# A two-layer typed graph transformer on one core: edge rows in a ring of 48 slots, one write behind each gather

## The chip, the core and the metric

The kernel runs on one core of a Trainium2 chip. The metric is device time in microseconds for one launch, the median of several runs. The core has five engines that work through their own queues in order: TensorE (PE), VectorE (DVE), ScalarE (ACT), GpSimd (POOL) and SyncE (SP). They meet at semaphores. Transfers between HBM and the on-chip memory SBUF run on 16 DMA engines; in this kernel every indexed transfer (a gather or a scatter with one row index per partition) is issued by POOL, every plain one inside the layers by SP. PSUM is the small memory that PE writes to and that DVE and ACT can read and write.

## What is computed

A graph of 6250 nodes and 100000 edges, 128 features, 8 heads of 16, 16 node types, 32 edge types, two layers:

```python
k, q, v = typed_linear(x, ntype, Wk), ...          # one 128x128 matrix per node type
kT = einsum('nhd,htdo->nhto', k, Watt)             # per node: a key for each edge type
vT = einsum('nhd,htdo->nhto', v, Wmsg)             # per node: a value for each edge type
kw, m = kT[src, :, etype], vT[src, :, etype]       # one row per edge
a = einsum('ehd,ehd->eh', kw, q[dst]) * pri[:, etype].T / SQRT_D
att = edge_softmax(a, dst, n)                      # softmax over the edges into a node
hag = segment_sum(m * att[:, :, None], dst)        # sum over the edges into a node
h = silu(typed_linear(hag, ntype, Wa))
h = layernorm(h * alpha + x * (1 - alpha)) * g + b
```

After two layers come a linear map, the residual with the input and a last normalisation.

## The kernel before

The keys and values of every node for all 32 edge types are written to a table in HBM, one for each layer (`tabs[l]`). A row of it holds 128 key values and 128 value values in f32, 1 KB. Nodes are sorted into 49 bins of 128 nodes, one node per partition, so that the nodes of a bin have about the same number of incoming edges. A bin has a fixed number of slots K (`KB`): 25, 21, 19, 18, 17, 16, 15, 15, 14, 12, 11 for the own bins of each of four groups of node types, and 42, 20, 16, 14, 9 for mixed bins. The slots of all bins add up to 833. Bins go by superblocks of two to four.

`edges(l)` does the attention of a layer. For each slot of a bin one gather on POOL (L1136) brings 128 table rows, one per partition. Behind each gather stand two small writes on POOL into a tile `pause` that nobody reads (L1140). POOL's order is the order in which the program is written; the other engines' queues are put in order by a scheduler. A chunk is a tile `kv` of up to four slots, out of twelve such tiles (48 slots of 1 KB per partition). For each chunk DVE multiplies the keys by the query in place (L1150) and sums each head (L1154) into `a`.

When all chunks of a bin are through, `finished` runs step by step between the chunks of the next bin: mask, maximum, exponential on ACT, denominator (L1042 to L1055), then for each chunk the values times the weights (L1066) and an addition into an accumulator of four rows (L1073), and at last the sum over these four rows (L1076). The accumulator, the weights and the query lie in SBUF in the first layer and in PSUM in the second. A tile `kv` is free for new gathers when its values are added.

`nodes` makes the rest of a superblock (normalisation of the sums L1188, transposes L231, typed linear maps L223 with masked inputs from DVE L209, layer norm), and in the first layer the keys, values and queries of the next one (L1302, L1283) and, through `table_block` (PE L246, copies on ACT L253 or DVE L251), the blocks of the second table, which POOL scatters to HBM (L1349), two scatters per bin. In the second layer POOL scatters the results (L1382). This work is put between the chunks: `step` advances `finished` by one step, `tick(n)` advances the work of earlier superblocks by the share that n slots stand for, `leave` counts the chunks until a result is written. Before, a chunk of c slots has three points with `step` and `tick(c / 3)`.

The second layer's first gather waits for all scatters of the table. The phase ahead of the layers sorts the edges, and makes the first table (scatters L893).

Of the kernel before, what the change touches and what calls it, by code (L numbers as in the profile page):

```python
# [9 lines left out]
F32 = mybir.dt.float32  # L10
BF16 = mybir.dt.bfloat16
# [17 lines left out]

BINS = P // NC  # L30

CH = 4


def bins_of_degrees(lam):
# [27 lines left out]
def kernel(  # L63
# [45 lines left out]
    assert max(KB) * H + P <= 512 and max(KB) <= P and min(KB) >= CH and NR >= NP and NB <= P and TY == NC * TC  # L109

    WIN = SB * P
    LO, HI = windows_of_types(N, NP - N, TY, WIN)
# [810 lines left out]
    def arm(fast):  # L923

        puts = []

        outs_put, results = [], []
        STB = 3 if fast else 2
        ep = ctx2.enter_context(tc.tile_pool(name="ep", bufs=2))
        npl = ctx2.enter_context(tc.tile_pool(name="npl", bufs=1))  # L930
        eps = npl.tile([P, 1], F32, name="eps")
        nc.vector.memset(eps, LN_EPS)

# [54 lines left out]
        def edges(l):  # L988
# [47 lines left out]
            def finished(s, i, chunks, kvt, a, pair, sums, den):  # L1036
# [12 lines left out]
                nc.vector.tensor_tensor(av, av, m.unsqueeze(1).to_broadcast([P, K, H]),  # L1049
                                        op=ALU.subtract)  # L1050
                w = av if l == 0 else pair[:, 1, D:D + K * H].rearrange("p (k h) -> p k h", h=H)
                nc.scalar.activation(w, av, AF.Exp)
                yield
                yield
                nc.vector.tensor_reduce(den[:, i, :], w.rearrange("p k h -> p h k"),  # L1055
                                        axis=AX.X, op=ALU.add)

                if l == 0:
                    acc = ep.tile([P, CH, D], F32, name="acc", bufs=1)
                else:  # L1060
                    acc = pair[:, 0].rearrange("p (k c) -> p k c", k=CH)
                for j in range(len(chunks) + 1):
                    if j < len(chunks):
                        j0, j1 = chunks[j]
                        v = kvt[j][:, :j1 - j0, D:]
                        nc.vector.tensor_tensor(  # L1066
                            (v if j else acc).rearrange("p k (h d) -> p k h d", h=H),
                            v.rearrange("p k (h d) -> p k h d", h=H),
                            w[:, j0:j1, :].unsqueeze(3).to_broadcast([P, j1 - j0, H, HS]),
                            op=ALU.mult)  # L1070
                    if j > 1:
                        j0, j1 = chunks[j - 1]
                        nc.vector.tensor_tensor(acc[:, :j1 - j0], kvt[j - 1][:, :j1 - j0, D:],  # L1073
                                                acc[:, :j1 - j0], op=ALU.add)
                    yield
                nc.vector.tensor_reduce(sums[:, i, :], acc.rearrange("p k c -> p c k"),  # L1076
                                        axis=AX.X, op=ALU.add)
# [13 lines left out]
            def table(s, gen):  # L1091
# [5 lines left out]
                else:  # L1097
                    tables[s] = gen
                    spread(pieces, gen, 8 * sbs[s][1] + 4, (1.0 if s + 4 < len(sbs) else 0.6) * slots(min(s + 2, len(sbs) - 1)))

            before = iter(())
            q, pair = query(0, 0)
            for s, (i0, k, types) in enumerate(sbs):
# [7 lines left out]
                for i in range(k):  # L1111
                    b = i0 + i
                    K = KB[b]
                    a = ep.tile([P, max(KB), H], F32, name="a")
                    chunks = [(j, min(j + CH, K)) for j in range(0, K, CH)]
                    kvt = []
                    then = []

                    def step(end=False):
# [9 lines left out]
                    for j0, j1 in chunks:  # L1129
                        c = j1 - j0  # L1130
                        kv = ep.tile([P, CH, 2 * D], F32, name="kv", bufs=12)
                        kvt.append(kv)
                        pause = ep.tile([P, CH, 2, SB * H], F32, name="pause", bufs=2)
                        for j in range(j0, j1):
                            at = KO[b] + j
                            get = nc.gpsimd.indirect_dma_start(  # L1136
                                out=kv[:, j - j0, :], out_offset=None, in_=tabs[l][:],
                                in_offset=bass.IndirectOffsetOnAxis(ap=ell[:, at:at + 1], axis=0))
                            for half in range(2):
                                nc.gpsimd.memset(pause[:, j - j0, half], 0.0)  # L1140
# [8 lines left out]
                        kk = kv[:, :c, :D]  # L1149
                        nc.vector.tensor_tensor(  # L1150
                            kk, kk, q.unsqueeze(1).to_broadcast([P, c, D]), op=ALU.mult)
                        step()
                        tick(c / 3)
                        nc.vector.tensor_reduce(a[:, j0:j1, :],  # L1154
                                                kk.rearrange("p k (h d) -> p k h d", h=H),
                                                axis=AX.X, op=ALU.add)
# [9 lines left out]
                    before = finished(s, i, chunks, kvt, a, pair, sums, den)  # L1166
                    q, pair = then[0] if then else (None, None)
            for _ in before:
                pass
# [53 lines left out]
        def nodes(l, i0, k, types, sums, den, ntb, table):  # L1223
# [326 lines left out]
```

## Time and profile before

Three runs took 3612.12, 3613.41 and 3602.87 us. The profiled execution took 3602.11 us, with a span of 3600.3 us.

| engine | busy us | share of the span | instructions |
|---|---|---|---|
| PE | 1776.3 | 49% | 5529 |
| DVE | 1905.3 | 53% | 4273 |
| ACT | 981.2 | 27% | 1599 |
| POOL | 2444.3 | 68% | 5483 |

How to read what follows. A row of a group names the line, the engine, the operation, what is written and read, the shape and the count; behind the bar stand the busy time in us and the mean of one instruction in ns; behind the second bar the time that the engine stood idle just before these instructions, and what ended it. "issue" is idle time in which nothing that the profile shows was waited for. A row of waits gives the total in us, the number of waits and the longest. A row of the timeline gives start, duration, engine, line and operation, with the idle time ahead of it in brackets. A row of a stage gives its limits and length in us, then busy time and count for PE, PE's weight loads, DVE, ACT and POOL, the granted clock of PE, the share of the DMA engines and GB/s.

### The profile page before, as it was taken

How to read it: one execution, taken by the hardware profiler on the slowest of the kernel's cores; microseconds unless marked ns; L12 is line 12 of the kernel's file. 1: busy time of each engine (PE TensorE's matmuls, PEld its weight loads, DVE VectorE, ACT ScalarE, POOL GpSimd, SP SyncE). 2: the span in 40 equal slices, each digit the busy share in tenths (PEclk: the TensorE clock that was granted, in tenths of full speed). 3: DMA queues.
4: the chain of work that ended last, by engine and by line, in shares of the span. 5: the costliest groups of instructions: out<-in, count | busy, mean ns of one | idle time of the engine just before them, and what ended most of it. 6: DMA issues, size and time to landing. Idle time of an engine off the chain costs nothing. (4 is left out here: it accounts for less than half of the span.)

```text
span 3600.3 us, 25278 instructions
## 1 busy us (share of the span) xinstructions
PE 1776.3 (49%) x5529; PEld 810.8 (23%) x5529; DVE 1905.3 (53%) x4273; ACT 981.2 (27%) x1599; POOL 2444.3 (68%) x5483
## 2 busy tenths in 40 slices
PE   4899889501775676546776669201201202113013
PEld 2455344300221232222222223101101101111012
DVE  8647423146544564446555552346556555556554
ACT  1556556300432243212342336101111101111111
POOL 1222466588688866688688771588888878888883
PEclk8769777555766686566776667655555555555555
DMA  5678899943655665354685569533333333333331
GB/s 139 289 303 338 334 378 411 356 100 95 222 205 207 236 237 214 133 205 147 218 321 185 179 245 363 203 94 102 98 99 98 100 88 103 97 97 98 99 97 39
DMA packets 189545, 681.72 MB, mean 189 GB/s; under 512 B 53964, under 2 KB 103278, under 8 KB 164334
## 3 DMA queue, kind: packets, MB, share of 16 engines
q0 software_dynamic: 115456, 642.08, 49.6%
q1 hardware_dynamic: 57538, 30.77, 3.2%
q10 hardware_dynamic: 16384, 7.11, 0.9%
q8 instruction: 48, 0.79, 0.1%
q14 instruction: 119, 0.97, 0.1%
HBM read 255.52 MB, written 425.02 MB: 189 GB/s over the span
## 5 line engine op out<-in xcount | busy, mean ns | idle before, releaser
L1136 POOL DMA_INDIRECT kv<-tab,ell x1666 | 1677.6, 1007 | 401.3 <-issue 303.4
L253 ACT COPY st<-tb 128x512 f32<-128x512 f32 (+1 forms) x1016 | 699.4, 758 | 671.2 <-PE tb L246 339.7
L231 PE MATMUL nb<-ident,hag 128*128 128x128 f32 x98 | 25.8, 406 | 754.1 <-DVE hag L1188 403.0
L1140 POOL MEMSET pause<- 128x32 f32 x3332 | 347.2, 141 | 40.7 <-issue 28.0
L1150 DVE TENSOR_TENSOR kv<-kv,tb 128x512 f32<-128x512 f32 (+3 forms) x227 | 145.4, 640 | 394.6 <-DMA kv<-tab,ell 382.5
L246 PE MATMUL tb<-bdv,kvT 32*128 32x512 f32 x784 | 290.6, 850 | 115.7 <-ACT st L253 69.0
L246 PE MATMUL tb<-bdk,kvT 32*128 32x512 f32 x784 | 280.6, 846 | 56.0 <-ACT st L253 34.9
L893 POOL DMA_INDIRECT tab<-st,rows x98 | 101.9, 1040 | 298.1 <-ACT st L253 232.2
L1154 DVE TENSOR_REDUCE a<-kv 128x32 f32<-128x512 f32 (+3 forms) x454 | 286.8, 635 | 3.6 <-DVE tb L1066 0.7
L246 PE MATMUL tb<-bdv,vT 32*128 32x512 f32 x784 | 275.8, 830 | 15.2 <-ACT st L253 8.0
L209 DVE SCALAR_TENSOR_TENSOR xm<-ntb,nb 128x512 f32<-128x512 bf16 (+2 forms) x288 | 157.5, 585 | 220.8 <-remote 66.0
L1150 DVE TENSOR_TENSOR kv<-kv,q 128x512 f32<-128x512 f32 (+3 forms) x227 | 145.4, 643 | 230.6 <-DMA kv<-tab,ell 220.0
L1349 POOL DMA_INDIRECT tab<-st,row x98 | 106.5, 1087 | 221.0 <-ACT st L253 186.5
L223 PE MATMUL nb<-xm,wa 128*128 128x512 f32 (+2 forms) x320 | 192.3, 752 | 112.8 <-DVE xm L209 73.3
L246 PE MATMUL tb<-bdk,kT 32*128 32x512 f32 x784 | 232.5, 825 | 1.5 <-ACT st L253 0.7
L251 DVE COPY st<-tb 128x512 f32<-128x512 f32 (+1 forms) x160 | 116.5, 730 | 210.1 <-PE tb L246 164.5
L231 PEld LDWEIGHTS nb<-ident,hag 128*128 128x128 f32 x98 | 15.9, 202 | 773.3 <-issue 598.8
L223 PE MATMUL nb<-xm,wq 128*128 128x512 f32 (+2 forms) x160 | 98.7, 765 | 156.9 <-DVE a L1042 91.9
L231 PE MATMUL nb<-ident,hs 128*128 128x128 f32 x98 | 36.0, 462 | 232.8 <-DVE hs L1261 174.3
L1302 PE MATMUL nb<-xm,wkqv 128*128 128x512 f32 (+1 forms) x288 | 144.7, 660 | 9.0 <-DVE xm L209 9.0
L1033 ACT COPY tb<-q 128x128 f32<-128x128 f32 x49 | 13.2, 269 | 454.2 <-DVE sums L1076 280.7
L246 PEld LDWEIGHTS tb<-bdv,kvT 32*128 32x128 f32 x784 | 79.7, 237 | 243.1 <-ACT st L253 134.4
(284 smaller groups left out, 2924.9 us busy)
## 6 DMA issues: line engine op xcount, KB each, us to landing
kv<-tab,ell POOLq DMA_INDIRECT x1666
hr<-xrd SPq DMA_DIRECT2D x24, 256.0 KB
hr<-xrd SPq DMA_DIRECT2D x15, 192.0 KB
xrd<-xr POOLq DMA_DIRECT2D x10, 256.0 KB
ntb<-typed SPq DMA_DIRECT2D x16, 128.0 KB
hrd<-hs SPq DMA_DIRECT2D x8, 256.0 KB
qrd<-q SPq DMA_DIRECT2D x8, 256.0 KB
q<-qrd SPq DMA_DIRECT2D x8, 256.0 KB
```

The costliest lines, as they stand in the source:

```text
L209: nc.vector.scalar_tensor_tensor(xm[:, :n], ntb[:, :n], float(t), hT[:, :n], op0=ALU.is_equal, op1=ALU.mult)
L223: nc.tensor.matmul(ps[:, :n], w[:, t, :], xm[:, :n], start=(t == types[0]), stop=(t == types[-1]))
L246: nc.tensor.matmul(pt[:, b], yT[s, i * P:(i + 1) * P], bd[s, tt, :], start=True, stop=True)
L251: nc.vector.tensor_copy(to, pt)
L253: nc.scalar.copy(to, pt)
L893: put = nc.gpsimd.indirect_dma_start(out=tabs[0].rearrange("(n t) c -> n (t c)", t=16), out_offset=bass.IndirectOffsetOnAxis(ap=rows1[:, t ...
L1136: get = nc.gpsimd.indirect_dma_start(out=kv[:, j - j0, :], out_offset=None, in_=tabs[l][:], in_offset=bass.IndirectOffsetOnAxis(ap=ell[:, ...
L1140: nc.gpsimd.memset(pause[:, j - j0, half], 0.0)
L1150: nc.vector.tensor_tensor(kk, kk, q.unsqueeze(1).to_broadcast([P, c, D]), op=ALU.mult)
L1154: nc.vector.tensor_reduce(a[:, j0:j1, :], kk.rearrange("p k (h d) -> p k h d", h=H), axis=AX.X, op=ALU.add)
L1302: nc.tensor.matmul(ps[:, :n], wkqv[:, j, t, :], xm[:, :n], start=(t == types[0]), stop=(t == types[-1]))
L1349: put = nc.gpsimd.indirect_dma_start(out=tabs[1].rearrange("(n t) c -> n (t c)", t=16), out_offset=bass.IndirectOffsetOnAxis(ap=row2[:, tg ...
```

## The change

Edge rows now lie in one tile `rows` of 48 slots that is used as a ring. `cut` divides a bin's K slots into chunks as even as can be, of at most eight, and cuts a chunk where the ring ends. `unread` holds the slots whose values are not yet summed; before a gather is written into such a slot, `finished` of the bin before is advanced. In `finished` each chunk's weighted values are summed over their slots by one instruction into a row of `part`, and the rows of `part` are summed at the end, in SBUF in both layers. A chunk has five points with `step` and `tick(c / 5)`. Behind each gather stands one write of 64 bf16 elements instead of two of 32 f32. Result rows are written after 4 + i chunks, not 7 + 2 i.

```diff
-CH = 4
+CH = 8
+RING = 48
...
+            ring["rows"] = npl.tile([P, RING, 2 * D], F32, name="rows")
...
-                if l == 0:
-                    acc = ep.tile([P, CH, D], F32, name="acc", bufs=1)
-                else:
-                    acc = pair[:, 0].rearrange("p (k c) -> p k c", k=CH)
-                for j in range(len(chunks) + 1):
-                    if j < len(chunks):
-                        j0, j1 = chunks[j]
-                        v = kvt[j][:, :j1 - j0, D:]
-                        nc.vector.tensor_tensor(
-                            (v if j else acc).rearrange("p k (h d) -> p k h d", h=H),
-                            v.rearrange("p k (h d) -> p k h d", h=H),
-                            w[:, j0:j1, :].unsqueeze(3).to_broadcast([P, j1 - j0, H, HS]),
-                            op=ALU.mult)
-                    if j > 1:
-                        j0, j1 = chunks[j - 1]
-                        nc.vector.tensor_tensor(acc[:, :j1 - j0], kvt[j - 1][:, :j1 - j0, D:],
-                                                acc[:, :j1 - j0], op=ALU.add)
-                    yield
-                nc.vector.tensor_reduce(sums[:, i, :], acc.rearrange("p k c -> p c k"),
+                part = ep.tile([P, PARTS, D], F32, name="part", bufs=1)
+                for j, (j0, j1, v, sl) in enumerate(chunks):
+                    nc.vector.tensor_tensor(
+                        v.rearrange("p k (h d) -> p k h d", h=H),
+                        v.rearrange("p k (h d) -> p k h d", h=H),
+                        w[:, j0:j1, :].unsqueeze(3).to_broadcast([P, j1 - j0, H, HS]),
+                        op=ALU.mult)
                     yield
+                    nc.vector.tensor_reduce(part[:, j, :], v.rearrange("p k c -> p c k"),
+                                            axis=AX.X, op=ALU.add)
+                    unread.difference_update(sl)
+                    yield
+                nc.vector.tensor_reduce(sums[:, i, :],
+                                        part[:, :len(chunks)].rearrange("p k c -> p c k"),
                                         axis=AX.X, op=ALU.add)
...
+            def cut(K):
+                cuts, j = [], 0
+                while j < K:
+                    most = -(-(K - j) // -(-(K - j) // CH))
+                    c = min(most, RING - ring["at"])
+                    sl = range(ring["at"], ring["at"] + c)
+                    cuts.append((j, j + c, ring["rows"][:, sl.start:sl.stop, :], sl))
+                    ring["at"] = sl.stop % RING
+                    j += c
+                return cuts
...
-                    chunks = [(j, min(j + CH, K)) for j in range(0, K, CH)]
+                    chunks = cut(K)
...
-                        kv = ep.tile([P, CH, 2 * D], F32, name="kv", bufs=12)
-                        pause = ep.tile([P, CH, 2, SB * H], F32, name="pause", bufs=2)
+                        while not unread.isdisjoint(sl):
+                            step()
+                        unread.update(sl)
+                        pause = ep.tile([P, CH, SB * BINS // 2], BF16, name="pause", bufs=2)
...
-                            for half in range(2):
-                                nc.gpsimd.memset(pause[:, j - j0, half], 0.0)
+                            nc.gpsimd.memset(pause[:, j - j0], 0.0)
...
-                        step()
-                        tick(c / 3)
+                        for _ in range(2):
+                            step()
+                            tick(c / 5)
                         nc.vector.tensor_reduce(a[:, j0:j1, :],
...
-                        step()
-                        tick(c / 3)
-                        step()
-                        tick(c / 3)
+                        for _ in range(3):
+                            step()
+                            tick(c / 5)
...
-                    results.append([7 + 2 * i, (o, i0, i)])
+                    results.append([4 + i, (o, i0, i)])
```

More of the change, by code (lines that the diff above doesn't have):

```diff
@@ L108 @@
     assert D == P and H * HS == D and H == 8 and HS == 16 and EC % J == 0 and NP > N and L == 2
-    assert max(KB) * H + P <= 512 and max(KB) <= P and min(KB) >= CH and NR >= NP and NB <= P and TY == NC * TC
+    assert max(KB) * H + P <= 512 and max(KB) <= P and RING >= max(KB) and NR >= NP and NB <= P and TY == NC * TC
     WIN = SB * P
@@ L927, in arm @@
         outs_put, results = [], []
+        PARTS = -(-max(KB) // CH) + 1
         STB = 3 if fast else 2
@@ L930, in arm @@
         npl = ctx2.enter_context(tc.tile_pool(name="npl", bufs=1))
+        ring = {"at": 0}
+        if fast:
+            ring["rows"] = npl.tile([P, RING, 2 * D], F32, name="rows")
         eps = npl.tile([P, 1], F32, name="eps")
@@ L1034, in query, with finished @@
                 return pair[:, 1, :D], pair
-            def finished(s, i, chunks, kvt, a, pair, sums, den):
+            def finished(s, i, chunks, a, pair, sums, den):
                 i0, k, _ = sbs[s]
@@ L1099, in table @@
                     spread(pieces, gen, 8 * sbs[s][1] + 4, (1.0 if s + 4 < len(sbs) else 0.6) * slots(min(s + 2, len(sbs) - 1)))
+            def cut(K):
[7 more added lines that the diff above has]
+                    j += c
+                assert len(cuts) <= PARTS
+                return cuts
+            unread = set()
             before = iter(())
@@ L1127, in step @@
                                 then.append(query(s + 1, 0))
-                    for j0, j1 in chunks:
+                    for j0, j1, kv, sl in chunks:
                         c = j1 - j0
-                        kv = ep.tile([P, CH, 2 * D], F32, name="kv", bufs=12)
-                        kvt.append(kv)
-                        pause = ep.tile([P, CH, 2, SB * H], F32, name="pause", bufs=2)
+                        while not unread.isdisjoint(sl):
+                            step()
+                        unread.update(sl)
+                        pause = ep.tile([P, CH, SB * BINS // 2], BF16, name="pause", bufs=2)
                         for j in range(j0, j1):
@@ L1165, in edges @@
                         step(end=True)
-                    before = finished(s, i, chunks, kvt, a, pair, sums, den)
+                    before = finished(s, i, [(j0, j1, kv[:, :, D:], sl) for j0, j1, kv, sl in chunks],
+                                      a, pair, sums, den)
                     q, pair = then[0] if then else (None, None)
```

3 lines of the change are left out of this document (1 added, 2 removed).

## The prediction

> **What bounds the kernel now.** I read the page's shares first, then busy time by stage, then POOL's groups and waits in each stage, then the timeline of a few gathers. The trace gives four stages from the kernel's lines: the first layer's gathers (704 to 2177 us), the table scatters left after them, the second layer's gathers (2293 to 3542), and the tail.
>
> ```profile
> span 3600.3 us, 25278 instructions
> ...
> POOL 1222466588688866688688771588888878888883
> ...
> 704.00:2177.00 1473.00, 877.36 (x2320) 338.86 (x2321) 800.80 (x1694) 423.69 (x563) 1135.48 (x2578) 0.66 0.58 197
> 2177.00:2293.00 116.00, 91.63 (x344) 35.87 (x342) 29.69 (x56) 67.03 (x82) 18.95 (x20) 0.75 0.90 369
> 2293.00:3542.00 1249.00, 215.43 (x538) 124.11 (x538) 696.26 (x1664) 130.45 (x263) 1015.10 (x2539) 0.53 0.33 97
> 3542.00:3600.00 58.00, 23.16 (x63) 14.73 (x63) 23.68 (x82) 11.26 (x17) 7.35 (x10) 0.53 0.05 16
> ```
>
> The columns are PE, PE's weight loads, DVE, ACT and POOL busy time. In the second layer POOL is busy 1015 of 1249 us and DVE 696; nothing else comes near. POOL's groups there, then in the first layer:
>
> ```profile
> L1136 POOL DMA_INDIRECT kv<-tab,ell x833 | 799.9, 960 | 197.4 <-issue 160.9 <-DMA tab<-st,row 9.0 <-DVE tb L1066 7.5
> L1140 POOL MEMSET pause<- 128x32 f32 x1664 | 174.9, 140 | 31.4 <-issue 24.4 <-POOL pause L1140 0.2
> ...
> L1136 POOL DMA_INDIRECT kv<-tab,ell x833 | 877.8, 1054 | 203.9 <-issue 142.5 <-DVE acc L1066 40.4 <-SPq L1546 8.8
> L1140 POOL MEMSET pause<- 128x32 f32 x1666 | 172.1, 142 | 9.3 <-issue 3.6 <-remote 3.6 <-POOL pause L1140 0.2
> L1349 POOL DMA_INDIRECT tab<-st,row x79 | 88.0, 1114 | 129.3 <-ACT st L253 113.7 <-issue 11.6 <-ACT a L1052 3.9
> ```
>
> In the second layer the first two groups with their idle time make 1204 of the 1249 us, and most of that idle time (185 of 229) is "issue", not another engine: POOL's instruction stream sets this stage. In the first layer 114 us pass while its scatters wait for ACT's table copies. There PE (877 of 1473 us) and ACT make the tables, and POOL is only one of two paces.
>
> **The change part by part.** *The write behind a gather.* A gather now repeats like this:
>
> ```profile
> 2401.21 0.20 POOL L1140 MEMSET pause<- 128x32 f32 x2
> 2401.57 0.95 POOL L1136 DMA_INDIRECT kv<-tab,ell  x1 [0.15 <-issue]
> 2402.52 0.21 POOL L1140 MEMSET pause<- 128x32 f32 x2
> 2402.88 0.95 POOL L1136 DMA_INDIRECT kv<-tab,ell  x1 [0.15 <-issue]
> ```
>
> So 0.95 + 0.20 + 0.15 = 1.31 us from gather to gather. Two writes of 0.14 overlap to 0.20: the second costs only 0.06. The trace also has gathers with no write between them, and longer writes:
>
> ```profile
> 102.62 0.97 POOL L847 DMA_INDIRECT xg<-in_x_dram,inv  x1 [0.30 <-issue]
> 103.89 0.95 POOL L847 DMA_INDIRECT xg<-in_x_dram,inv  x1 [0.30 <-issue]
> 105.14 0.95 POOL L847 DMA_INDIRECT xg<-in_x_dram,inv  x1 [0.30 <-issue]
> ...
> L858 POOL MEMSET kT<- 128x197 f32 x1 | 0.3, 278 | 0.0
> ```
>
> Without any write the step is 1.25 us: 0.30 passes between two gathers anyhow, and the writes stand mostly inside it. One write as long as now gives 0.95 + 0.14 + 0.15 = 1.24, or that 1.25. But the one write is 64 bf16 elements, not 32 f32 (the same 128 bytes), and no bf16 write on POOL is in the trace. If elements count and not bytes, it costs (278 - 140) / (197 - 32) = 0.84 ns for each of 32 more, 0.167 us, and the step is 1.27. The ends are therefore 0.04 and 0.07 us saved; I take 0.055, between the two. Per layer that is 833 x 0.055 = 46 us (33 to 58).
>
> The Trainium skill (VectorE: DVE Perf Modes, Zero memsets can be issued as uint32) says that a memset costs a cycle per element whatever the type, on VectorE; if POOL followed it, the write would be the longer one and this term 33 us a layer instead of 46. No run here shows it yet.
>
> *Fewer instructions on POOL.* Beyond the regular 0.154 us, "issue" holds irregular stalls, such as this one:
>
> ```profile
> 2419.84 0.12 POOL L1140 MEMSET pause<- 128x32 f32 x1 [0.18 <-issue]
> 2420.55 0.13 POOL L1140 MEMSET pause<- 128x32 f32 x1 [0.58 <-issue]
> 2421.45 0.95 POOL L1136 DMA_INDIRECT kv<-tab,ell  x1 [0.78 <-issue]
> ...
> POOL kv L1136 <- issue: 160.9, 724, 1.5
> POOL pause L1140 <- issue: 24.4, 62, 1.3
> ...
> POOL kv L1136 <- issue: 142.5, 778, 1.5
> POOL tab L1349 <- ACT st L253: 113.7, 20, 19.6
> POOL kv L1136 <- DVE acc L1066: 40.4, 3, 23.6
> ```
>
> Layer two (first two waits): 160.9 - 724 x 0.154 + 24.4 = 74 us; layer one: 142.5 - 778 x 0.154 + 3.6 = 26 us. I don't know what they wait for. If they come by the number of instructions, one of three instructions per gather goes and a third of the stalls (25 and 9 us); if by time or by gather, nothing. I take half of that: 12 and 4 us.
>
> *The ring.* Before, a bin of 42 rows takes 11 of the 12 tiles of four, which leaves 4 rows of lead; now 48 - 42 = 6, given back by chunk. In the order of the two programs, the gather with the shortest lead over the gather on whose sums it waits has a lead of 1 in the second layer before (its wait on DVE is the 7.5 us above) and 7 after; most others have 14 or more in both. In the first layer the shortest lead is 5 before and 3 after (the 49th gather, once). So the ring takes away the 7.5 us in the second layer (0 to 9), and about nothing in the first; the 40.4 us there come from a DVE that itself stands behind PE, which the ring doesn't touch:
>
> ```profile
> 1389.41 0.56 DVE L209 SCALAR_TENSOR_TENSOR xm<-ntb,nb 128x384 f32<-128x384 bf16 x1 [14.49 <-PE tb L246]
> ```
>
> The table scatters come one or two gathers later in POOL's order, the result writes about five earlier: no cost.
>
> *VectorE.* The two layers have 454 chunks before and 271 after, over the same 1666 rows of 128 values.
>
> ```profile
> L1154 DVE TENSOR_REDUCE a<-kv 128x32 f32<-128x512 f32 x376 | 254.8, 678 | 2.3 <-DVE a L1049 0.3 <-DVE kv L1066 0.3
> L1154 DVE TENSOR_REDUCE a<-kv 128x8 f32<-128x128 f32 x26 | 7.3, 279 | 0.1
> L1076 DVE TENSOR_REDUCE sums<-acc 128x128 f32<-128x512 f32 x49 | 51.3, 1048 | 1.2 <-DVE hs L1261 0.9
> L1076 DVE TENSOR_REDUCE sums<-tb 128x128 f32<-128x512 f32 x49 | 33.4, 682 | 1.3 <-DVE t L1205 1.3
> L1073 DVE TENSOR_TENSOR tb<-kv,tb 128x512 f32<-128x512 f32 (+3 forms) x174 | 109.5, 629 | 0.0
> L1073 DVE TENSOR_TENSOR acc<-kv,acc 128x512 f32<-128x512 f32 (+3 forms) x176 | 110.1, 626 | 0.3
> ```
>
> From the first two rows an instruction costs 0.146 us and 1.04 ns per element. The sum over rows of acc in SBUF, which steps from row to row, costs (1048 - 146) / 512 = 1.76 ns; from PSUM it costs the plain rate. The new sum of a chunk steps through SBUF in both layers. Per layer it costs 833 x 128 x 1.76 ns + 135 x 0.146 = 208 us (131 at the plain rate); the sum over the parts adds about 38. Out go the adds (110), the old last sum (50 and 33) and 3 x 91 x 0.146 = 40 of fixed cost. DVE so has about 46 us more in the first layer and 63 in the second. At 696 + 63 = 759 us of some 1180 it stays well under POOL, and the lead of 14 rows (18 us) covers its lateness: cost nothing. If that cover went, the 63 us would be the price.
>
> The Trainium skill (SBUF — State Buffer, SBUF "cachelines") speaks against this edit: accesses that go to a new 16-byte line each time pay a penalty in SBUF. By it the longer step of 1 KB costs no more than acc's 512 bytes, since both change line on every element, and the sum is the 208 us that the row gives.
>
> *Gathers held up by DVE (first layer).* Gathers there take 877.8 us, where 833 x 0.955 would be 796: 82 us more. The trace shows when: a gather that starts while two-input DVE instructions on SBUF run back to back.
>
> ```profile
> 1545.99 1.29 DVE L1066 TENSOR_TENSOR kv<-kv,a 128x512 f32<-128x512 f32 x2
> 1546.30 4.82 POOL L1136 DMA_INDIRECT kv<-tab,ell  x1 [0.15 <-issue]
> 1547.19 0.69 DVE L1073 TENSOR_TENSOR acc<-kv,acc 128x512 f32<-128x512 f32 x1
> ...
> 1549.60 0.69 DVE L1073 TENSOR_TENSOR acc<-kv,acc 128x512 f32<-128x512 f32 x1
> ```
>
> The adds, which make these trains long, become reductions with one input; but the multiplies that stay are nearly twice as long each. I take 10 us of gain, between 40 (the long trains gone) and a loss of 10.
>
> *The sum.* Second layer 46 + 12 + 7 = 65 us (33 to 92). First layer 46 + 4 + 10 = 60 us on POOL (23 to 107); scatters wait for ACT 20 times in it, and after each such wait what POOL had gained is gone if PE and ACT are as late as before. I keep half, 30 us (0 to 107). The drain of 116 us is PE and ACT, the tail of 58 a chain over all engines: nothing. Together 95 us. The profiled execution took 3602.1 us (1.8 more than its span), so 3507; the median of the runs shown is 10 above that execution, and I predict 3510 for a median.
>
> **The rivals.**
> - *All of the first layer's gain is kept* (POOL sets that stage too). For it: waits on ACT are 114 of 1473 us and PE is busy only 60%. Against: PE's work hangs on sums that come at the same points of the order. 3602 - 65 - 60 = 3477; with half of what the better ends add (27 and 47), 3440.
> - *None of it is kept*: each us that POOL gains comes back as a wait for table copies. 3602 - 65 = 3537; with the worse end of the second layer 3570, as a median about 3580.
> - *The write doesn't matter*: one write of 64 elements leaves the step near 1.31 (it would have to cost 0.20), and the stalls stay. 3602 - 7 = 3595. The row of 278 ns for 197 elements speaks against it.
> - *Slower: the first layer's VectorE stands longer.* DVE takes its instructions in order, and a multiply now waits for up to eight gathers; behind it stand the masked inputs that PE waits for.
>
> ```profile
> DVE kv L1150 <- DMA kv<-tab,ell: 220.0, 76, 9.9
> ...
> PE nb L223 <- DVE xm L209: 77.7, 27, 11.7
> ```
>
> If the 220 us of standing grow by half, to 330, and the 46 us above come on top, the tables end 156 us later and the time is 3602 + 156 - 65 = 3693. It turns the sign when the first layer grows by 65 us, 0.5 us for each of its 135 chunks. Against it: there are fewer such stands (135, not 227), five points per chunk at which other work is put in, and the step from gather to gather is shorter.
>
> **How the numbers follow.** Likeliest 0.50 (3480 to 3540 for it alone); all kept 0.15; none kept 0.20; the write doesn't matter 0.05; slower 0.10. The range, 3440 to 3580, holds the first three with their ends. About 0.3% (11 us) is what a measurement of this kernel can tell from no change. Faster 0.85, same 0.05, slower 0.10.
>
> **What would show it.** In the second layer: gather to gather 1.25 to 1.27 us instead of 1.31, the stage near 1185 us, "issue" per gather up from 0.15 if the writes' time is only partly saved; no wait on DVE of several us. The chunk's sum at about 1.95 us for 1024 elements (1.2 would be the plain rate). In the first layer: waits of the scatters on ACT at 130 to 150 us, gathers near 868 us in sum. I am wrong if the step stays at 1.31, if DVE's waits for gathers rise in sum in the first layer and the drain starts later than 2177 us, or if POOL waits for DVE in many places.

## The result, and the profile after

The changed kernel took 3640.3 us (3624.75 to 3658.1), the kernel before 3613.41 us (3593.64 to 3625.52) on the same chip: a ratio of 1.0086, with an interval of 1.0067 to 1.0105. Forecast was 3510. The change made the kernel a little slower.

The span of the profiled execution, from its page:

```profile
span 3638.0 us, 22799 instructions
```

The two layers, bounded here by the first and last gather of each, first before, then after (limits, length, then busy time of PE, its weight loads, DVE, ACT and POOL, clock, DMA share, GB/s). What lies between a kernel's two rows is the drain, in which the last scatters of the table are written:

```profile
704.00:2162.00 1458.00, 862.64 (x2278) 333.40 (x2278) 790.92 (x1677) 416.69 (x554) 1133.59 (x2575) 0.66 0.58 198
2293.00:3541.00 1248.00, 215.43 (x538) 124.11 (x538) 695.26 (x1660) 130.45 (x263) 1014.25 (x2538) 0.53 0.33 97
```

```profile
703.00:2187.00 1484.00, 859.62 (x2290) 336.94 (x2292) 841.35 (x1373) 417.59 (x557) 1079.15 (x1743) 0.66 0.57 194
2309.00:3575.00 1266.00, 221.25 (x538) 125.75 (x538) 752.61 (x1344) 129.80 (x263) 976.55 (x1706) 0.53 0.33 96
```

POOL did get less to do: 54 us less in the first layer, 38 in the second. But it stood idle 80 us longer in the first (405 against 324) and 56 longer in the second (289 against 234). So the layers grew by 26 and 18 us. The regular step became shorter, as the timeline of the changed kernel's POOL shows:

```profile
2342.44 0.95 POOL L1152 DMA_INDIRECT rows<-tab,ell  x1 [0.16 <-issue]
2343.39 0.17 POOL L1155 MEMSET pause<- 128x64 bf16 x1
2343.72 0.95 POOL L1152 DMA_INDIRECT rows<-tab,ell  x1 [0.16 <-issue]
```

From gather to gather it is 1.28 us instead of 1.31. All of this gain and more POOL lost in waits. First those of before in the first and in the second layer, then those of the changed kernel in the first, and then in the second:

```profile
POOL tab L1349 <- ACT st L253: 104.4, 19, 19.6
...
POOL kv L1136 <- DVE tb L1066: 7.5, 1, 7.5
POOL out_dram L1382 <- DVE o L1335: 4.9, 3, 2.3
```

```profile
POOL rows L1152 <- issue: 162.5, 809, 2.2
POOL tab L1365 <- ACT st L255: 151.3, 23, 19.4
POOL rows L1152 <- DVE part L1072: 46.3, 4, 21.3
POOL tab L1365 <- ACT rs L1214: 14.5, 1, 14.5
```

```profile
POOL rows L1152 <- issue: 206.7, 811, 2.1
POOL out_dram L1398 <- DVE o L1351: 24.2, 3, 9.8
POOL pause L1155 <- issue: 14.8, 39, 0.9
POOL rows L1152 <- DVE hs L1266: 10.7, 1, 10.7
POOL rows L1152 <- DVE rs L1225: 6.8, 1, 6.8
```

In the first layer the table scatters wait 47 us more for ACT (151.3 against 104.4) and 14.5 once for ACT's `rs`. In the second, results and rows that DVE delivers late make 42 us (24.2 + 10.7 + 6.8), where the rows of before have 12 (7.5 + 4.9). A part of "issue" is the regular 0.163 us per gather now; what goes beyond it is 206.7 - 811 x 0.163 + 14.8 = 89 us in the second layer (74 before) and, with 3.5 at the writes, 162.5 - 809 x 0.163 + 3.5 = 34 in the first (26 before). These irregular stalls did not shrink with POOL's instructions; they grew.

DVE's waits tell where the lateness comes from. Before, in the first and in the second layer:

```profile
DVE xm L209 <- remote: 73.1, 18, 13.9
...
DVE kv L1150 <- DMA kv<-tab,ell: 382.5, 128, 17.7
DVE bn L1217 <- remote: 91.9, 10, 13.3
```

The changed kernel, first and second layer:

```profile
DVE rows L1165 <- DMA rows<-tab,ell: 131.6, 33, 9.6
DVE xm L211 <- remote: 116.5, 17, 22.2
...
DVE rows L1165 <- DMA rows<-tab,ell: 231.1, 45, 21.4
DVE bn L1233 <- remote: 136.8, 11, 19.2
```

DVE's waits for gathers fell (they were 220.0 and 382.5 us). "remote" rose: here a semaphore that an engine waited for was raised at a time when no instruction of another engine had just ended. One such wait in the timeline of the changed kernel:

```profile
2784.95 0.80 PE L1344 MATMUL nb<-hr,ident 128*128 128x128 f32 x2
...
2797.28 0.36 SPq L965 DMA_DIRECT2D hr<-xrd  x1
2797.29 0.89 DVE L1233 BATCH_NORM_STATS2 bn<-nb 128x6 f32<-128x128 f32 x4 [15.61 <-remote]
```

PE's last matmul into `nb` ends at 2785.75. DVE, which reads `nb`, and SP, which may overwrite `hr`, both go on at 2797.28, and the trace has the update of PE's semaphore at 2797.27: PE's signal reached them 11.5 us late. Meanwhile DVE, bound to its order, summed nothing.

### The profile page after: what moved, and what is told of

Its sections match the earlier page's. It is cut to its first block, busy times and chain, and to the rows that moved or that the text cites. A ratio compares the mean times of both kernels' runs of the same rounds, so it can differ in the third digit from the quotient of the medians.

```text
span 3638.0 us, 22799 instructions
## 1 busy us (share of the span) xinstructions
PE 1767.2 (49%) x5529; PEld 805.8 (22%) x5529; DVE 2011.8 (55%) x3639; ACT 980.0 (27%) x1599; POOL 2350.6 (65%) x3817
## 5 line engine op out<-in xcount | busy, mean ns | idle before, releaser
L1152 POOL DMA_INDIRECT rows<-tab,ell x1666 | 1653.3, 992 | 468.8 <-issue 370.0
L1072 DVE TENSOR_REDUCE part<-rows 128x128 f32<-128x896 f32 (+6 forms) x271 | 392.9, 1466 | 11.7 <-remote 6.3
L248 PE MATMUL tb<-bdv,kvT 32*128 32x512 f32 x784 | 272.4, 822 | 121.7 <-issue 64.6
L1155 POOL MEMSET pause<- 128x64 bf16 x1666 | 279.0, 167 | 24.8 <-issue 18.4
L1165 DVE TENSOR_TENSOR rows<-rows,tb 128x768 f32<-128x768 f32 (+7 forms) x136 | 131.4, 966 | 273.3 <-DMA rows<-tab,ell 231.1
L1170 DVE TENSOR_REDUCE a<-rows 128x56 f32<-128x896 f32 (+6 forms) x271 | 261.0, 965 | 6.1 <-issue 1.8
L253 DVE COPY st<-tb 128x512 f32<-128x512 f32 (+1 forms) x160 | 116.5, 729 | 202.2 <-PE tb L248 174.9
L1165 DVE TENSOR_TENSOR rows<-rows,q 128x768 f32<-128x768 f32 (+6 forms) x135 | 131.8, 977 | 157.1 <-DMA rows<-tab,ell 131.6
L1318 PE MATMUL nb<-xm,wkqv 128*128 128x512 f32 (+1 forms) x288 | 155.0, 697 | 35.0 <-DVE xm L211 25.6
L1058 ACT ACTIVATE tb<-a 128x120 f32<-128x120 f32 (+12 forms) x49 | 14.1, 288 | 522.9 <-DVE a L1055 305.1
L225 PEld LDWEIGHTS nb<-xm,wa 128*128 128x128 f32 x320 | 83.8, 286 | 254.3 <-DVE xm L211 126.8
```

Of the source, the lines that this page charges most:

```text
L225: nc.tensor.matmul(ps[:, :n], w[:, t, :], xm[:, :n], start=(t == types[0]), stop=(t == types[-1]))
L248: nc.tensor.matmul(pt[:, b], yT[s, i * P:(i + 1) * P], bd[s, tt, :], start=True, stop=True)
L253: nc.vector.tensor_copy(to, pt)
L1072: nc.vector.tensor_reduce(part[:, j, :], v.rearrange("p k c -> p c k"), axis=AX.X, op=ALU.add)
L1152: get = nc.gpsimd.indirect_dma_start(out=kv[:, j - j0, :], out_offset=None, in_=tabs[l][:], in_offset=bass.IndirectOffsetOnAxis(ap=ell[:, ...
L1155: nc.gpsimd.memset(pause[:, j - j0], 0.0)
```

## The experiments

The chips on which the kernels below ran are of two sorts. The kernel before takes 3366 us on two of them (called quick chips here) and 3585, 3605 and 3608 us on three others (plain chips); the one of the result, at 3613, is of the second sort. Each ratio is against the kernel before on the same chip; it is worked out over all the runs, so it is not exactly the quotient of the two medians. In the expectations G stands for the chunks of eight delaying the first layer, S for the cost of the strided sums on DVE, B and W for gains of POOL that come back as waits, C for a loss that hangs on the chip, and R for a shorter step that makes signals late.

### Parts of the change on a quick chip

*e1: before with the one write of 64 bf16.*

```diff
-pause = ep.tile([P, CH, 2, SB * H], F32, name="pause", bufs=2)
+pause = ep.tile([P, CH, SB * BINS // 2], BF16, name="pause", bufs=2)
-for half in range(2):
-    nc.gpsimd.memset(pause[:, j - j0, half], 0.0)
+nc.gpsimd.memset(pause[:, j - j0], 0.0)
```

> The kernel before with one write of 64 bf16 elements behind each gather; all else as before. Theory G (grain): the single write saves 0.03 us per gather (1.31 to 1.28), and the loss of the changed kernel comes from chunks of eight, in which several steps of the other work stand in a row on DVE and DVE waits for PE and ACT between them. Theory S (strided sum): the loss comes from the 112 us of DVE work that the sum through SBUF adds. Theory B (given back): POOL is not what sets the end, and every us that it gains comes back as a wait, whatever the chunks are. G and S: 3565 to 3590. B: 3605 to 3620.

*e2: the changed kernel with the two writes of 32 f32 put back* (its `pause` is then one tile of 2 KB).

```diff
-pause = ep.tile([P, CH, SB * BINS // 2], BF16, name="pause", bufs=2)
+pause = ep.tile([P, CH, 2, SB * H], F32, name="pause", bufs=1)
-nc.gpsimd.memset(pause[:, j - j0], 0.0)
+for half in range(2):
+    nc.gpsimd.memset(pause[:, j - j0, half], 0.0)
```

> The changed kernel with two writes of 32 f32 elements behind each gather, as before the change (their tile has one buffer, for space). G and S: the step is 1.31 again and the losses of the changed kernel stay, 3660 to 3690. B: 3630 to 3650, no slower than the changed kernel.

*e3: the changed kernel in chunks of four, with the three points and the place of the result writes of before* (its ring has 46 slots).

```diff
-CH = 8
-RING = 48
+CH = 4
+RING = 46
-for _ in range(2):  step(); tick(c / 5)
+step(); tick(c / 3)
-for _ in range(3):  step(); tick(c / 5)
+for _ in range(2):  step(); tick(c / 3)
-results.append([4 + i, (o, i0, i)])
+results.append([7 + 2 * i, (o, i0, i)])
```

> The changed kernel with chunks of at most four, three points for other work per chunk and results after 7 + 2 i chunks, as before the change; ring (46 slots, for space), strided sum and the one write as in the changed kernel. G: the losses go, 3560 to 3595. S: they stay, 3630 to 3650. B: about 3613.

*e4: before with one write of 32 f32.*

```diff
-for half in range(2):
-    nc.gpsimd.memset(pause[:, j - j0, half], 0.0)
+nc.gpsimd.memset(pause[:, j - j0, 0], 0.0)
```

> The kernel before with the first of its two writes alone (32 f32 elements). If a write costs by elements, the step is 1.25 us and the time is lower than with one write of 64 bf16: G and S 3545 to 3575. B: 3605 to 3620.

Before: 3366.09 us. e1 3328.76, ratio 0.9891 (0.9876 to 0.9906); e2 3350.72, 0.9954 (0.9938 to 0.9971); e3 3302.65, 0.9817 (0.9801 to 0.9833); e4 3282.98, 0.9753 (0.9734 to 0.9772). On this chip no part of the change loses time against before. The ring gains 26 us in chunks of four (e3 against e1) and 15 in chunks of eight (e2 against before), so the longer chunks may give back some 10 us, too little to turn the sign. The timeline of e4's POOL:

```profile
2400.52 0.95 POOL L1136 DMA_INDIRECT kv<-tab,ell  x1 [0.17 <-issue]
2401.48 0.14 POOL L1139 MEMSET pause<- 128x32 f32 x1
2401.78 0.95 POOL L1136 DMA_INDIRECT kv<-tab,ell  x1 [0.17 <-issue]
```

The write of 32 elements takes 0.14 us and the step 1.256; that of 64 takes 0.17 and the step 1.281. Elements count on POOL, not bytes, which is what the Trainium skill (VectorE: DVE Perf Modes, Zero memsets can be issued as uint32) says of VectorE. e4's step saves 1666 x 0.056 = 93 us, of which 83 are kept; e1's saves 52, of which 37 are kept. So on such a chip the step sets the time, B fails, and S too, since e2 has the strided sums and is faster.

### The changed kernel and shorter writes on a plain chip

*e5: the changed kernel again. e6: the changed kernel with one write of 32 f32. e7: e3 with one write of 32 f32.* In e6 and e7:

```diff
-pause = ep.tile([P, CH, SB * BINS // 2], BF16, name="pause", bufs=2)
+pause = ep.tile([P, CH, SB * H], F32, name="pause", bufs=2)
```

> The changed kernel itself, beside the kernel before on the chip that this call gets. The second layer's irregular stalls of POOL make 77 us in the kernel before and 87 us in the changed kernel on the chip of the result; on the chip of the first four experiments they are all but absent, and the kernel before takes 3366 us there. Theory C (chip): the changed kernel loses only where the engines stall irregularly. Where the kernel before takes about 3366, the changed kernel then takes 3310 to 3335; where it takes about 3613, 3630 to 3650. Theories G and S: no faster than the kernel before on either chip.

> The changed kernel with one write of 32 f32 elements in place of 64 bf16. The step is 1.256 instead of 1.281 us: 0.025 x 1666 = 42 us if POOL sets both layers, so 20 to 42 us below the changed kernel of the same call. If POOL's gains are given back (theory B), within 8 us of it.

> Ring of 46 slots, chunks of at most four with three points each, strided sum, and one write of 32 f32 elements. With the step at 1.256 us, 0.970 to 0.976 of the kernel before on a chip without the stalls (the same kernel with 64 bf16 elements had 0.9817). On a chip with them: theory G 0.975 to 0.990; if the stalls alone make the changed kernel's loss, about 1.0.

Before: 3605.23 us. e5 3647.78, ratio 1.0099 (1.0063 to 1.0136); e6 3647.55, 1.0116 (1.0079 to 1.0152); e7 3678.65, 1.0185 (1.0141 to 1.0228). e6's step is 1.256 us, 0.025 less than e5's, and that is worth nothing. e7 has chunks of four and is the slowest, so G fails here. Its DVE waits in the first layer:

```profile
DVE xm L211 <- remote: 150.4, 12, 25.2
DVE rows L1165 <- DMA rows<-tab,ell: 92.6, 33, 8.9
```

DVE waits less for gathers here than in any of the other kernels so far (131.6 us in the changed kernel). Its row of late signals is longer than the changed kernel's (116.5 us), but that of e6, a faster kernel on the same chip, is longer still (188.2 us), so this row by itself doesn't tell the time.

### The same four on a plain chip

*e8: the changed kernel. e9: as e1. e10: as e4. e11: as e3.*

> The changed kernel once more, beside three others on one chip. The kernel before takes 3366 us on some chips and 3605 to 3613 us on others; on the slower ones semaphores reach the engines late during the gathers and the changed kernel is 0.9 to 1.0 per cent slower. Theory C (the change shortens the path, and loses only where signals come late): on a chip of 3366 us 0.980 to 0.990 of before, since the ring in chunks of four with the same write gave 0.982; on a chip of 3610 us 1.009 to 1.011. Theory S (the strided sums and the long chunks cost VectorE, whatever the chip): 1.00 or more on both.

> The kernel before with the one write of 64 bf16 alone (step 1.281 us instead of 1.312; 0.989 of before on a chip of 3366 us). On a chip of 3610 us: theory W (there a shorter step is given back in full as waits, whatever else changes) 0.997 to 1.003, and the ring carries the whole loss of the change; theory R (the shorter step itself draws more late signals) 1.003 to 1.010; if nothing hangs on the chip, 0.987 to 0.991.

> The kernel before with one write of 32 f32 alone (step 1.256 us; 0.975 of before on a chip of 3366 us). On a chip of 3610 us: theory W 0.997 to 1.003; theory R 1.005 to 1.015, more than the write of 64 elements; if nothing hangs on the chip, 0.973 to 0.978.

> The ring of 46 rows in chunks of four with one write of 64 bf16 (0.982 of before on a chip of 3366 us). On a chip of 3610 us: theory W 1.000 to 1.010; if the chunks of eight carry the loss, 0.985 to 0.995; if nothing hangs on the chip, 0.980 to 0.984. On a chip of 3366 us, beside the changed kernel: theory G (chunks of eight delay the first layer) has the changed kernel 0.5 to 1 per cent longer than this one, otherwise both are equal within 0.4 per cent.

Before: 3584.56 us. e8 3606.8, ratio 1.0079 (1.0045 to 1.0114); e9 3630.26, 1.0133 (1.0093 to 1.0173); e10 3633.41, 1.0144 (1.0110 to 1.0179); e11 3623.84, 1.0123 (1.0086 to 1.0160). The shorter write alone, in the otherwise unchanged kernel, makes it 1.3 to 1.4% slower on this chip, where the very same program was 1.1 and 2.5% faster on the quick one. W, which had it at 0.997 to 1.003, falls; R holds in sign, though e9's loss is above its 1.010 and no smaller than e10's. The two layers of one program, e1 on the quick chip and then e9 on the plain one:

```profile
712.00:2007.00 1295.00, 821.32 (x2301) 330.70 (x2302) 797.15 (x1687) 416.87 (x559) 1093.93 (x1743) 0.69 0.65 221
2129.00:3268.00 1139.00, 204.93 (x538) 122.97 (x538) 693.07 (x1657) 130.16 (x262) 980.14 (x1707) 0.54 0.36 107
```

```profile
707.00:2175.00 1468.00, 849.66 (x2278) 330.60 (x2278) 789.86 (x1675) 414.77 (x554) 1092.54 (x1741) 0.66 0.57 196
2303.00:3565.00 1262.00, 218.86 (x538) 124.03 (x538) 701.83 (x1643) 126.37 (x256) 977.49 (x1707) 0.53 0.33 96
```

POOL, DVE and ACT are busy nearly the same time on both; 173 and 123 us are idle time of theirs that the plain chip adds. PE is busy 28 and 14 us longer there, at a granted clock of 0.66 instead of 0.69 and 0.53 instead of 0.54, which is far less than what is added. Until the first gather both take the same (712 and 707 us). DVE's waits in the second layer, e1, then e9:

```profile
DVE kv L1149 <- DMA kv<-tab,ell: 394.7, 158, 17.5
DVE bn L1216 <- PE nb L1327: 31.3, 11, 4.2
```

```profile
DVE kv L1149 <- DMA kv<-tab,ell: 199.0, 74, 6.6
DVE bn L1216 <- remote: 109.2, 8, 21.5
```

The wait of `bn` for PE's `nb` is 31 us in all and at most 4.2 on the quick chip; on the plain chip the longest is 21.5 and its cause is no instruction's end. How late signals are can be worked out from the trace's record of semaphores: for each recorded update the time since the latest end of an instruction that makes one on that engine's semaphore. The longest of PE in the first layer, and for DVE in the second layer the number of records over 1 us late and the sum of those over 0.4 us late:

```
chip   kernel                        step us   PE, longest   DVE over 1 us   sum, us
quick  e1  before, one write 64       1.281      0.1 us        0 of 1617         0
quick  e14 ring, two writes           1.31       0.1           0 of 1325         0
plain  e18 before, one write 128      1.336      9.4          63 of 979        165
plain  before, two writes             1.312     11.1          27 of 789         77
plain  e17 ring, two writes           1.31      15.4           9 of 665         23
plain  after, one write 64            1.281     25.8          43 of 708        119
plain  e16 after again                1.281     26.8          47 of 680        124
plain  e9  before, one write 64       1.281     22.1         112 of 1017       280
plain  e10 before, one write 32       1.256     23.7          98 of 970        263
```

In no trace from a quick chip is a signal of PE or DVE more than 0.13 us late while gathers run. On the plain ones they are, nearly all while gathers run (before the first gather PE's are at most 2.5 us late), and with one short write PE's latest are about twice as late as with two. (e14, e16, e17 and e18 follow below.) The counts differ because the plain chips' record is not complete: DVE's instructions make 4024 updates in the program of e1 and e9, of which 4023 are recorded in e1 and 2989 in e9; PE's make 2476, of which 2475 and 2111 are. The instructions themselves are all there. A record that is missing makes no other one look late, since each is measured from the latest end before it, but shares of late ones can't be compared from chip to chip.

### Third and fourth writes

*e12: before with three writes. e13: with four. e15: the changed kernel with three. e14: as e2.* The further writes go to the same elements. e12's edit is shown; e13 has `(0, 1, 0, 1)` there:

```diff
-for half in range(2):
+for half in (0, 1, 0):
     nc.gpsimd.memset(pause[:, j - j0, half], 0.0)
```

> The kernel before with a third write of 32 f32 behind each gather. The step should grow from 1.312 to about 1.37 us (each further write 0.06). Theory R (a shorter step makes the engines' semaphore updates late): on a chip of 3585 to 3610 us PE's updates in the first layer come within 5 to 8 us for 99 of 100 instead of 8.6, and the time is 0.985 to 1.003 of before, although POOL has 100 us more to do. Theory W (late signals have another cause, POOL's gains were given back as waits): 1.005 to 1.03. On a chip of 3366 us, where no signal is late, 1.020 to 1.030 (0.87 of 100 us, as with the shorter steps).

> The kernel before with four writes of 32 f32 behind each gather: step about 1.43 us. Theory R on a chip of 3585 to 3610 us: updates less late again, under 5 us for 99 of 100 of PE's in the first layer; 0.98 to 1.02 of before. Theory W: 1.03 to 1.06. On a chip of 3366 us 1.045 to 1.06.

> The changed kernel with the two writes of 32 f32 put back (0.995 of before on a chip of 3366 us). On a chip of 3585 to 3610 us: theory R, since the step is that of before, 0.990 to 1.000, and PE's updates as late as before; if the ring carries the loss, 1.005 to 1.015.

> The changed kernel with three writes of 32 f32: step about 1.37 us. On a chip of 3585 to 3610 us: theory R 0.98 to 1.00; theory W or the ring as the cause 1.01 to 1.03. On a chip of 3366 us 1.015 to 1.025.

This was again a quick chip. Before: 3365.84 us. e12 3739.91, ratio 1.1108 (1.1089 to 1.1128); e13 3829.42, 1.1370 (1.1348 to 1.1391); e15 3710.52, 1.1018 (1.0997 to 1.1039): some 8% above what was expected. e12's POOL:

```profile
2902.84 0.32 POOL L1140 MEMSET pause<- 128x32 f32 x3
2903.74 0.95 POOL L1136 DMA_INDIRECT kv<-tab,ell  x1 [0.58 <-issue]
2904.70 0.32 POOL L1140 MEMSET pause<- 128x32 f32 x3
2905.16 0.95 POOL L1136 DMA_INDIRECT kv<-tab,ell  x1
```

The third write costs 0.12 us, not 0.06; it overwrites the first and carries a wait for POOL's own signal, as 1666 of the 4998 writes do. And ahead of 138 gathers of the first layer and 161 of the second POOL stands some 0.43 us longer than ahead of the others (0.576 for 0.148), 128 us in all. Whether these stalls come from the waits I didn't take apart, and no signal is late here (PE's at most 0.1 us), so these three say nothing of a longer pause where signals are late. e14 took 3350.87 us, 0.9954 (0.9937 to 0.9972), the same as e2: on quick chips the ring, its sums and its chunks of eight are worth 15 us.

### The pause on a plain chip

*e16: the changed kernel. e17: as e2. e18: before with one longer write.*

```diff
-pause = ep.tile([P, CH, 2, SB * H], F32, name="pause", bufs=2)
+pause = ep.tile([P, CH, 4 * SB * H], F32, name="pause", bufs=1)
-for half in range(2):
-    nc.gpsimd.memset(pause[:, j - j0, half], 0.0)
+nc.gpsimd.memset(pause[:, j - j0], 0.0)
```

> The changed kernel. On a chip where the kernel before takes 3366 us, by theory C (a gain that is lost where signals come late): 0.980 to 0.988 of before, 0.995 for the ring with two writes less the 0.011 that the write of 64 bf16 gave by itself; if chunks of eight lose what the step gains, 0.995 or more. On a chip of 3585 to 3610 us 1.007 to 1.011 as before.

> The changed kernel with the two writes put back: 0.995 on a chip of 3366 us. On a chip of 3585 to 3610 us: theory R (the shorter step makes the signals late, and the ring costs nothing) 0.985 to 1.000; if the ring carries a loss of its own, 1.005 to 1.015.

> The kernel before with one write of 128 f32 behind each gather in place of two of 32: one instruction fewer, but a longer step, about 1.335 us instead of 1.312. On a chip of 3366 us, where the step sets the time: 1.007 to 1.013. On a chip of 3585 to 3610 us: theory R (the rate of the gathers makes the signals late) 0.98 to 1.00, and PE's updates in the first layer less late than before's 8.6 us for 99 of 100; if it is the second write itself that helps there, and not the time it takes, 1.01 to 1.02.

Before: 3608.16 us. e16 3651.05, ratio 1.0107 (1.0074 to 1.0139); e17 3571.76, 0.9906 (0.9872 to 0.9940); e18 3589.57, 0.9964 (0.9939 to 0.9990). e16 and e17 differ in the writes behind the gather (and the tile that they go to) alone; their layers:

```profile
713.00:2203.00 1490.00, 860.46 (x2288) 339.28 (x2288) 840.11 (x1372) 417.78 (x557) 1075.48 (x1742) 0.66 0.57 194
2325.00:3592.00 1267.00, 212.70 (x538) 122.48 (x538) 752.37 (x1344) 129.61 (x263) 978.05 (x1706) 0.53 0.33 96
```

```profile
710.00:2136.00 1426.00, 869.87 (x2292) 341.50 (x2292) 841.40 (x1372) 417.75 (x557) 1102.73 (x2575) 0.67 0.59 202
2258.00:3508.00 1250.00, 215.00 (x545) 126.08 (x545) 754.41 (x1356) 131.23 (x266) 1009.68 (x2539) 0.53 0.33 97
```

With the second write POOL works 27 and 32 us more, and the layers are 64 and 17 us shorter. e18's step, from its timeline, is longer than before's 1.312:

```profile
2400.99 0.95 POOL L1136 DMA_INDIRECT kv<-tab,ell  x1 [0.17 <-issue]
2401.95 0.22 POOL L1139 MEMSET pause<- 128x128 f32 x1
2402.33 0.95 POOL L1136 DMA_INDIRECT kv<-tab,ell  x1 [0.17 <-issue]
```

It is 1.34 us, 40 us more over both layers, and yet e18 is 0.4% faster than before, with one write only. So what helps is the time between gathers, not the second write as an instruction. The trace of e18 is of an execution of 3614 us, one of its slowest, so it can't show where the median of 3590 gains. In it PE's signals in the first layer were a little less late (99 of 100 within 7.5 us, 8.6 before), in the second later (up to 24 us, 8.5 before). Two rows of POOL's waits in it, over the whole run:

```profile
POOL kv L1136 <- issue: 281.0, 1601, 1.5
POOL pause L1139 <- remote: 41.7, 17, 4.3
```

With 5.9 us at the writes, the irregular part of "issue" is 281.0 - 1601 x 0.165 + 5.9 = 23 us in both layers, against 123 in the changed kernel (34 + 89) and 100 before (26 + 74). e18 has as few instructions on POOL as the changed kernel (3817), so these stalls don't go by their number. (Nor do those of e9, the same kernel with the write of 64 and as many instructions: 335.3 - 1571 x 0.163 + 13 = 92 us, on another plain chip.) They don't set the time alone either: e17, the fastest here, has 289.6 - 1551 x 0.155 + 25.7 = 75 us of them and 67 of "remote" at its writes. e17 is the version that beat the kernel before on both sorts of chip.

## Why the prediction was wrong

**The step that failed** is the largest term of the sum, "the write behind a gather": 46 us a layer, taken as time saved because "POOL's instruction stream sets this stage", with the waits of POOL left as they were. The step did become shorter, by 0.031 us, but on a plain chip shortening it costs more than it saves. e9 makes this edit alone: by the forecast's rule it gains 46 us in the second layer and half of that in the first, and it lost 46 us (3584.56 to 3630.26). The pair e16 and e17, which differ in the writes alone, shows it by layer: POOL has 27 and 32 us less to do with the shorter write, and the layers are 64 and 17 us longer.

What the runs showed in its place is waits that the shorter step draws. Over a whole run the scatters of the second table wait for ACT's copies 187 us in the kernel before, 181 in e17 and 172 in e18, but 226 in the changed kernel, 218 in e16 and 222 in e9 (112 in e1, on a quick chip). PE's latest signals in the first layer are 9 to 15 us late in the three traces from plain chips without a short single write, and 22 to 28 us in the nine with one. So the late signals of PE rise with the time, and that they turn the saved time into a loss is read from the traces; no experiment moved them without moving the step or the chip. DVE's in the second layer don't follow the time as well: e18 has more of them than the kernel before.

The trace before had "remote" waits of DVE and ACT in both layers (DVE's longest rows are 73.1 and 91.9 us), and I put no price on their growing. The smaller term "fewer instructions on POOL" was wrong with it: I bounded the change of the irregular stalls between a third saved and nothing saved and took 12 and 4 us of gain, and they grew by 15 and 8 us. e18 shows that they don't go by the number of instructions, which was the case that I gave the third for.

**The write.** I took 46 us per layer; the step fell by 0.031 us, 26 us. The write itself took 0.166 us, my upper case (0.167), and the 0.163 us behind it, where I had put 0.15, took the rest. On a quick chip e1 kept 37 of the 52 us.

**The ring and the sums.** Together I gave them 17 us (7 for the wait, 0 for VectorE, 10 for the gathers). e2 and e14 have 15 us, e17 36. Right in sign on both sorts of chip, and small where signals are on time. DVE's cost was sized well. The row of the commonest chunk, from the changed kernel's groups:

```profile
L1072 DVE TENSOR_REDUCE part<-rows 128x128 f32<-128x768 f32 x100 | 143.7, 1444 | 3.6 <-DVE rows L1066 1.6 <-DVE a L1170 1.1 <-DVE part L1072 0.6
```

That is (1444 - 146) / 768 = 1.69 ns per element, where I took 1.76, and DVE is busy 50 and 57 us more in the two layers, where I took 46 and 63.

**The first layer's gathers.** They take 855.5 us in sum instead of 877.8, 22 us less where I took 10.

**Half of the first layer's gain kept.** There was no gain: it grew by 26 us on the plain chip, and the scatters wait 166 us for ACT (151.3 + 14.5), where I had said 130 to 150. On the quick chip e14's first layer is 1312 us and e17's 1426, for one program.

**Drain and tail.** The drain was 122 us instead of 131, the tail (from the last gather to the end of the span) 63 instead of 59: together nothing, as said. The forecast's own sum gives 3517 for a median, 10 above 3507, where I wrote 3510; nothing hangs on that.

**The rivals.** The slower one had the sign right and the mechanism wrong. DVE's waits for gathers fell, from 220.0 to 131.6 us in the first layer, and chunks of four (e7, e11) lose as much as chunks of eight. "The write doesn't matter" is wrong on both sorts of chip: there it gains, here it loses. "All of the first layer's gain is kept" is out, since that layer grew. "None of it is kept" is nearest to what e6 shows, where a step shorter by 0.025 us moved nothing.

**What stays open.** The changed kernel was not run on a quick chip; from e2 (0.9954) and e1 (0.9891) it should take about 0.985 there, or 3315 us, an estimate. What makes the signals late, and why only on some chips, isn't known: the packets of the queue that carries the gathers take as long on both (median 159 ns in each layer in e1 and e9). The recording of the profile may take part, since it is on the chips with late signals that records of updates are missing; all the times here come with it, so no run can tell.

## What to carry to other kernels

A pause behind a DMA issue may be doing work: before taking one away, look whether the other engines wait for signals that no instruction's end explains, and price the change by their waits too, not by the issuing engine's time alone. Try such an edit by itself and on more than one chip, since a gain of 2.5% on one was a loss of 1.4% on another. Keep what pays on all: here the ring without the shorter write.

## What was unexpected of the hardware

The kernel before took 3366 us on two chips and 3585 to 3613 on the others. One program (e1 and e9) had the same time until the first gather there, nearly the same busy times, and granted clocks of 0.651 and 0.633. On the slower ones a semaphore's update came up to 28 us after the instruction that made it (PE, first layer, e8 with one short write), against 0.1 us on the others, and a quarter of DVE's updates in e9 have no record at all. ACT's own recorded updates were on time on both (at most 0.01 us).
